# Two levels of Strassen for three quarters of the query projections, and values weighed by half blocks, in an attention kernel

## The chip, the core and the metric

The kernel runs on one core of a Trainium2 chip. The metric is device time in microseconds (us) of one launch. Engines: PE (TensorE matmul; PEld is its weight load, which overlaps it), DVE (VectorE), ACT (ScalarE), POOL (GpSimd), SP (SyncE, which here issues nearly all DMAs).

## What is computed

Eight batch entries of 256 tokens with 512 features, float32. After a layer norm, attention with 128 heads runs beside a gated FFN, and `x + s * g` is returned:

```python
c_q = x @ Wq_down                      # 512 -> 64
c_kv = x @ Wkv_down                    # 512 -> 64
q_c = (c_q @ Wq_up)                    # 128 heads of 4
q_r = (x @ Wq_rope)                    # 512 -> 128 heads of 64: the large projection
k_c, v_c = c_kv @ Wk_up, c_kv @ Wv_up  # 128 heads of 4 each
k_r = x @ Wk_rope                      # 64, shared by all heads
scores = (q_c . k_c + q_r . k_r) / scale
out = softmax(scores) @ v_c            # then out @ Wo
```

The rope queries `q_r` are a product of 2048 x 512 with 512 x 8192; it and the scores are most of the work.

## The kernel before

All instructions are recorded in the order in which the Python runs (a manual schedule), so each engine's queue has exactly that order; semaphores are put in wherever a tile is written or read by another engine. A first phase does layer norm, the low-rank projections and the FFN gate for all tokens, block of 512 by block of 512, and writes gates, sums and projections to DRAM. Then a loop runs over 64 blocks `n`. A block is one batch entry and one group of 16 heads (`sg`); batch entries go in pairs (four pairs of 16 blocks). Each block has two halves. The text calls half 0 even and half 1 odd, and counts halves h = 2n + half, from 0 to 127.

What one half does, in the order in which it is recorded:

- `score` twice (line 864): 4 PSUM banks each, 48 matmuls of 256 columns in row tiles of 32. With it all eight banks are given out; banks come round in turn, and a bank's next user waits for its last reader.
- `Prepare` in every second even half: the small query and key projections of the next blocks (lines 249 to 261).
- `maxima` (877, DVE, eight reductions), `exponentials` (883, ACT, 16 in a half).
- `Project`: one unit j of the rope queries. A unit is a 256 x 512 weight part times the pair's 512 tokens, by one level of Strassen: seven products of two 128-row chunks, each on four column tiles of 32 (`on_columns`, line 173), 56 matmuls of 256 columns, into four banks. `first` gives four products, ACT copies them out between the exponentials of the second part (line 211), POOL adds them (`join`, 216 to 218), `second` accumulates three more onto the emptied banks, and DVE adds the last (`end`, 228 and 229). Unit j = h + 4 is made in half h, four to six halves before the scores that use it.
- `transpose` (890, DVE, eight), into `rings`, four tiles with three parts of half a block each.
- DMAs for later units: `load_rope` (124, 512 KB), and `sum_w`. For the first pair, `sum_w` adds the weights' four Strassen sums on POOL (136 to 139) and stores them to DRAM (`sums_d`, 140); later pairs load them (142, 512 KB). The sums of x are in DRAM (`xs_d`), and `load_xs` brings seven of them when a pair begins (167).
- In even halves: `spread` (269, POOL, masks the small queries of the next block), `normalize` (953 to 955, DVE), `weigh` of the block before (915: 32 matmuls of 256 columns over the whole block), `gather` of its result by ACT (936) with two adds on POOL in blocks with odd `sg` (942), and `place_values` (310, POOL, four copies).

The few lines that set the order in the middle of a half:

```python
pj.first()
for r, i in enumerate((0, 2, 3, 1)):
    exponentials(n, two, r)
    pj.take(i)
if pre:
    pre.take()
pj.join()
pj.second()
```

Of the kernel before, what the change touches and what calls it, by code (L numbers as in the profile page):

```python
# [32 lines left out]
EPS = 1e-5  # L33
QSCALE = float((HD + R) ** -0.5)
# [3 lines left out]
def mla_ffn_gate_kernel(  # L38
# [26 lines left out]
    ident = const.tile([P, P], F32, name="ident")  # L65
    make_identity(nc, ident)
# [18 lines left out]
    sums_d = [dram.tile([P, 4, 2, P], F32, name=f"sums_d{n}") for n in range(32)]  # L85
    gates_d = [dram.tile([P, D], F32, name=f"gate_d{n}") for n in range(NT // P)]

    actp = pool("act", 4)
    wp = pool("wrope", 2)
# [3 lines left out]
    wsp = pool("wsum", 2)  # L93
    xsp = pool("xsum", 1)
    qtp = pool("qt", 1)
# [10 lines left out]
    units = 4 * len(blocks) // 2  # L106
    ropes, wsums, xsums = {}, {}, {}
# [10 lines left out]

    def load_rope(j):

        if j < units:
            t = wp.tile([P, KT, 4 * R], F32, tag="w", name=f"w_{j}")
            sg, u = j // 4 % 8, j % 4
            nc.sync.dma_start(out=t, in_=w_rope[sg, u // 2][:, :, ds(u % 2 * 4 * R, 4 * R)])
            ropes[j] = t

    def sum_w(j):  # L130

        if j < units:
            t = wsp.tile([P, 4, 2, P], F32, tag="ws", name=f"ws_{j}")
            if j < 32:
                q = lambda a, k: ropes[j][:, 2 * k : 2 * k + 2, a::2]
                nc.gpsimd.tensor_add(t[:, 0], q(1, 0), q(1, 1))
                nc.gpsimd.tensor_sub(t[:, 1], t[:, 0], q(0, 0))  # L137
                nc.gpsimd.tensor_sub(t[:, 2], q(0, 0), q(1, 0))
                nc.gpsimd.tensor_sub(t[:, 3], q(0, 1), t[:, 1])
                nc.sync.dma_start(out=sums_d[j], in_=t)  # L140
            else:
                nc.sync.dma_start(out=t, in_=sums_d[j % 32])
            wsums[j] = t

    def sum_x(p, xnT):


        q = lambda k, e: xnT[:, 2 * k : 2 * k + 2, ds(e * S, S)]
        for i, of in ((0, q(0, 0)), (1, q(1, 0)), (2, q(1, 1))):
            nc.sync.dma_start(out=xs_d[p][:, i], in_=of)  # L150
        t = {i: xsp.tile([P, 2, S], F32, tag=f"x{i}", name=f"xt{i}_{p}") for i in range(3, 7)}
        for i, one, two in (
            (3, q(0, 1), q(0, 0)),
            (4, q(1, 1), t[3]),
            (5, q(1, 1), q(0, 1)),
            (6, q(1, 0), t[4]),
        ):
            nc.gpsimd.tensor_sub(t[i], one, two)
            nc.sync.dma_start(out=xs_d[p][:, i], in_=t[i])

    def load_xs(p):

        if p < B // 2:
            xsums[p] = {}
            for i in (0, 4, 5, 3, 1, 6, 2):
                xsums[p][i] = xsp.tile([P, 2, S], F32, tag=f"x{i}", name=f"x{i}_{p}")
                nc.sync.dma_start(out=xsums[p][i], in_=xs_d[p][:, i])
# [12 lines left out]
    class Project:  # L180


        def __init__(self, j):
# [3 lines left out]
            self.a = lambda a, k: w[:, 2 * k : 2 * k + 2, a::2]  # L187
            self.x = xsums[j // 32]
# [4 lines left out]
            self.banks = []  # L193
            self.e = [qtp.tile([P, S], F32, tag=f"e{i}", name=f"e{i}_{j}") for i in range(4)]
# [7 lines left out]
        def first(self):  # L202

            for i, (w, x) in enumerate(
                ((self.a(0, 0), 0), (self.s[:, 1], 4), (self.s[:, 2], 5), (self.s[:, 0], 3))
            ):
                self.banks.append(bank(f"q{i}_{self.j}")[:, 0:S])
                product(self.banks[i], w, self.x[x], True)

        def take(self, i):  # L210
            nc.scalar.copy(self.e[i], self.banks[i])  # L211

        def join(self):

            m1, m6, m7, m5 = self.e
            nc.gpsimd.tensor_add(m6, m6, m1)  # L216
            nc.gpsimd.tensor_add(m7, m7, m6)  # L217
            nc.gpsimd.tensor_add(self.out(1, 1), self.split(m7), self.split(m5))  # L218

        def second(self):  # L220

            for i, w, x in ((0, self.a(0, 1), 1), (2, self.a(1, 1), 6), (3, self.s[:, 3], 2)):
                product(self.banks[i], w, self.x[x], False)
            nc.scalar.copy(self.out(0, 0), self.split(self.banks[0]))

        def end(self):

            nc.vector.tensor_add(self.out(1, 0), self.split(self.e[1]), self.split(self.banks[2]))  # L228
            nc.vector.tensor_add(self.out(0, 1), self.split(self.e[1]), self.split(self.banks[3]))

        def start(self):
            self.first()
            for i in (0, 2, 3, 1):
                self.take(i)
            self.join()
# [78 lines left out]
    def first_phase(between):  # L314
        st = ExitStack()
        fw = pool("fw", 1, st)
        wdn_sb = fw.tile([P, KT, P], F32, name="wdn_sb")
# [389 lines left out]
        for tb in range(NTB):  # L707
            more = tb + 1 < NTB
            for u in range(6):
# [9 lines left out]
                if pj:  # L719
                    pj.second()  # L720
                    pj.end()
# [20 lines left out]
            else:  # L742
                low_out(tb, 2)
                low_sum(tb)
            gate_out(tb)
# [48 lines left out]
    def between(step):  # L794
# [4 lines left out]
        elif step == 1:  # L799
            load_act(0)  # L800
            load_act(1)
            for b in range(2):
                load_cv(b, qtp.tile([P, S], F32, tag=f"e{b}", name=f"cv_{b}"))
            for j in range(2):
                load_rope(j)
        elif step == 2:
            load_xs(0)
# [8 lines left out]
        elif step < 8:  # L816
            load_rope(step - 2)
            if step < 6:
                sum_w(step - 2)
        else:  # L820
            sum_w(4)
            sum_w(5)
            load_act(2)
# [20 lines left out]
    rings = [tp.tile([P, 3, 8, 4, 32], F32, name=f"ring{r}") for r in range(4)]  # L844
# [43 lines left out]
    def transpose(n, f, r):  # L888

        nc.vector.transpose(  # L890
            rings[r][:, (2 * n + f // 2) % 3].rearrange("p k q i -> p q k i")[:, ds(2 * (f % 2), 2)],
# [4 lines left out]
    swapped = {}  # L896

    def weigh(n, halves=range(2)):
# [3 lines left out]
        if 0 in halves:  # L902
            avs[n] = bank(f"av_{n}")
        av = avs[n]
        slots = [(2 * n + half) % 3 for half in halves]
        if len(slots) == 2:
            one, two = sorted(slots)
            of, cols = slice(one, two + 1, two - one), ds(0, S)
            swapped[n] = one != slots[0]
        else:  # L910
            of, cols = slice(slots[0], slots[0] + 1), ds(halves[0] * P, P)
            swapped[n] = False
        for k in range(8):
            for r in range(4):
                nc.tensor.matmul(  # L915
                    av[32 * r : 32 * r + 32, cols],
                    vpad[:, k, r, :],
                    rings[r][:, of, k].rearrange("p h q i -> p h (q i)"),
# [5 lines left out]
    def gather(n, cols=ds(0, S)):  # L924


        b, sg = blocks[n]
        if n not in accs:
            accs[n] = [
                smp.tile([P, S], F32, tag=f"acc{what}{sg % 2}{b % 2}", name=f"acc{what}_{n}", bufs=1)  # L930
                for what in range(2)
            ]
        for what in (1, 0):
            side = (sg + what) % 2
            for to, of in ((early, late), (late, early)) if swapped[n] else ((cols, cols),):
                nc.scalar.activation(  # L936
                    accs[n][what][:, to], avs[n][:, of], AF.Copy, scale=sides_sb[:, side : side + 1]
                )
        if sg % 2:
# [64 lines left out]
    for n, (b, sg) in enumerate(blocks):  # L1004
        for half in range(2):
            one, two = 2 * half, 2 * half + 1
            j = 2 * n + half + 4
# [14 lines left out]
            if j < units:  # L1022
                pj = Project(j)
                pj.first()
                for r, i in enumerate((0, 2, 3, 1)):
# [142 lines left out]
```

## Time and profile before

| | |
|---|---|
| median of 3 runs | 1974.92 us (1974.73 to 1974.92) |
| profiled execution, span | 1971.5 us |
| PE busy | 1960.1 us (99%) |
| DVE busy | 1578.2 us (80%) |
| ACT busy | 1099.8 us (56%) |
| POOL busy | 758.5 us (38%) |
| DMA, mean over the span | 95 GB/s, 187 MB |
| PE busy by line: products (173, q) | 870.8 us |
| PE busy by line: scores (864) | 769.3 us |
| PE busy by line: weighing (915) | 233.4 us |

The profiler took one execution; its span runs from the first to the last instruction. "Busy" is time in which at least one instruction of the engine ran; register, semaphore and DMA-issuing instructions aren't counted. Matmuls are pipelined, so a mean duration (379 ns for a record of 256 columns) is longer than the distance from one start to the next. Each float32 matmul of the program stands in the trace as two records. In groups by shape, `128*32 128x256` is a weight tile of 128 rows and 32 columns and 256 columns that stream past it.

### The profile page before, as it was taken

The numbers are of one execution on the slowest core, as the hardware profiler recorded it, in microseconds if no ns is written. First come the engines' busy times: TensorE is split into PE (matmuls) and PEld (weight loads), VectorE is DVE, ScalarE is ACT, GpSimd is POOL, SyncE is SP. The second block draws the span as 40 slices with busy tenths as digits, with TensorE's granted clock in tenths as the row PEclk, the third lists the DMA queues.
The fourth block names the chain that finished last, engine by engine and source line by source line (L and its number), as shares of the span: only waits on it lengthen the run. The fifth ranks groups of instructions, "written<-read, shape, count | busy, mean of one in ns | idle before, by whom it ended". The sixth has DMA issues, their size and how long they took to land.

```text
span 1971.5 us, 78641 instructions
## 1 busy us (share of the span) xinstructions
PE 1960.1 (99%) x34007; PEld 1308.5 (66%) x34007; DVE 1578.2 (80%) x2662; ACT 1099.8 (56%) x3031; POOL 758.5 (38%) x1113
## 2 busy tenths in 40 slices
PE   9999999999999999999999999999999999999998
PEld 4335677677677666676777766776776767677675
DVE  7765678888887877888887877788787878888888
ACT  4433565655665644656655654556656555655664
POOL 6867445455443233233233223232233323233232
PEclk9999999999999999999999999999999999999999
DMA  6344322222242223222232223222232222122212
GB/s 196 114 135 168 118 88 72 83 88 77 77 135 90 77 101 113 75 88 88 67 125 87 81 88 122 80 88 78 76 123 72 98 88 88 67 88 88 83 39 87
DMA packets 120078, 187.02 MB, mean 95 GB/s; under 512 B 10778, under 2 KB 84906, under 8 KB 119734
## 3 DMA queue, kind: packets, MB, share of 16 engines
q1 hardware_dynamic: 119665, 181.97, 27.3%
q8 instruction: 270, 4.42, 0.9%
q14 instruction: 75, 0.61, 0.1%
q0 software_dynamic: 64, 0.01, 0.0%
q10 hardware_dynamic: 4, 0.01, 0.0%
HBM read 147.86 MB, written 34.10 MB: 92 GB/s over the span
## 4 chain that ended last, share of the span: by engine, by line
PE 93%; POOL 2%; DVE 2%; DMA 1%; issue 1%; SPq 1%; ACT 0%; POOLq 0%; ACTq 0%; DVEq 0%
PE q L173 39%; PE sc L864 34%; PE av L915 11%; PE po L173 2%; PE pf L173 1%; PE py L173 1%; PE px L173 1%; PE qq L249 1%; DVE ring L890 1%; PE pm L173 1%; PE pp L173 1%; DMA wo_sb<-in_w_o_dram 0%; PE first L656 0%; PE vps L294 0%; DVE nmx L877 0%
## 5 line engine op out<-in xcount | busy, mean ns | idle before, releaser
L883 ACT ACTIVATE pr<-sc,nmx 128x256 f32<-128x256 f32 x2048 | 816.5, 501 | 462.8 <-DVE nmx L877 458.6
L877 DVE TENSOR_REDUCE nmx<-sc 128x2 f32<-128x512 f32 x1024 | 635.8, 684 | 282.2 <-PE sc L864 257.6
L890 DVE STREAM_TRANSPOSE ring<-pr 128x512 f32<-128x512 f32 x1024 | 635.1, 679 | 0.0
L216 POOL TENSOR_TENSOR e<-e,e 128x256 f32<-128x256 f32 x128 | 93.7, 732 | 1043.1 <-ACT e L211 559.3
L173 PE MATMUL q<-x,ws 128*32 128x256 f32 x8192 | 489.1, 379 | 0.1
L864 PE MATMUL sc<-act,qr 32*128 32x256 f32 x8192 | 488.4, 374 | 0.0
L864 PEld LDWEIGHTS sc<-act,qr 32*128 32x128 f32 x8192 | 420.9, 185 | 21.8
L173 PEld LDWEIGHTS q<-x,ws 128*32 128x32 f32 x8192 | 267.5, 110 | 175.0 <-POOL ws L137 0.6
L173 PE MATMUL q<-x,w 128*32 128x256 f32 x6144 | 381.7, 381 | 1.1 <-DMA x<-xs_d 1.1
L173 PEld LDWEIGHTS q<-x,w 128*32 128x32 f32 x6144 | 188.3, 110 | 154.9 <-ACT pr L883 35.5
L864 PE MATMUL sc<-kc,qcm 32*128 32x256 f32 x4096 | 280.9, 387 | 0.0
L864 PEld LDWEIGHTS sc<-kc,qcm 32*128 32x128 f32 x4096 | 198.1, 184 | 65.0 <-issue 54.1
L915 PE MATMUL av<-ring,vpad 128*32 128x256 f32 (+1 forms) x4160 | 233.4, 376 | 0.1
L211 ACT COPY e<-q 128x256 f32<-128x256 f32 x512 | 204.0, 399 | 29.9 <-PE q L173 29.7
L936 ACT ACTIVATE acc<-av,sides_sb 128x128 f32<-128x128 f32 (+1 forms) x172 | 60.7, 421 | 243.9 <-PE av L915 243.9
L915 PEld LDWEIGHTS av<-ring,vpad 128*32 128x32 f32 x4160 | 134.3, 110 | 88.7 <-issue 1.6
L269 POOL TENSOR_TENSOR qcm<-qc,mask_sb 128x1024 f32<-128x1024 f32 x64 | 122.3, 1911 | 0.0
L218 POOL TENSOR_TENSOR qr<-e,e 128x256 f32<-128x256 f32 x128 | 93.6, 731 | 10.0
L217 POOL TENSOR_TENSOR e<-e,e 128x256 f32<-128x256 f32 x128 | 93.6, 731 | 10.0
L310 POOL COPY vpad<-vall 32x128 f32<-32x128 f32 x256 | 75.5, 295 | 10.2 <-PE av L915 2.2
L228 DVE TENSOR_TENSOR qr<-e,q 128x256 f32<-128x256 f32 x128 | 54.0, 422 | 24.3 <-POOL e L216 17.4
L568 DVE SCALAR_TENSOR_TENSOR gate<-low,bcol_sb,px 128x512 f32<-128x512 f32 x44 | 32.8, 746 | 44.6 <-PE px L173 21.5
(134 smaller groups left out, 1137.2 us busy)
## 6 DMA issues: line engine op xcount, KB each, us to landing
w<-in_w_rope_dram SPq DMA_DIRECT2D x128, 512.0 KB
ws<-sums_d SPq DMA_DIRECT2D x96, 512.0 KB
sums_d<-ws SPq DMA_DIRECT2D x32, 512.0 KB
x<-xs_d SPq DMA_DIRECT2D x28, 256.0 KB
xt<-in_x_dram SPq DMA_DIRECT2D x16, 256.0 KB
xs_d<-xt SPq DMA_DIRECT2D x16, 256.0 KB
gate_d<-gs SPq DMA_DIRECT2D x16, 256.0 KB
g<-gate_d SPq DMA_DIRECT2D x16, 256.0 KB
```

The source lines that it names most:

```text
L173: nc.tensor.matmul(to[tile_], w[:, tile_], x, start=start, stop=stop, skip_group_check=True)
L211: nc.scalar.copy(self.e[i], self.banks[i])
L216: nc.gpsimd.tensor_add(m6, m6, m1)
L217: nc.gpsimd.tensor_add(m7, m7, m6)
L218: nc.gpsimd.tensor_add(self.out(1, 1), self.split(m7), self.split(m5))
L269: nc.gpsimd.tensor_mul(qcm, qks[b, sg // 2][0].rearrange("p (q i) -> p q i", i=32).unsqueeze(2).to_broadcast([P, 8, 4, 32]), mask_sb[:, ds ...
L310: nc.gpsimd.tensor_copy(vpad[rows, :, :, 8 * t + 4 * (sg % 2) :][..., :4], valls[b][rows, :, sg])
L864: nc.tensor.matmul(sc[r][:, h, :], lhs.rearrange("p t i -> p (t i)"), rhs, start=(part == 0 and h == 0), stop=(part == 2), skip_group_chec ...
L877: nc.vector.tensor_reduce(nmx[:, r, :], scs[n, f][r], AX.X, ALU.max, negate=True)
L883: nc.scalar.activation(p[:, h, :], scs[n, f][r][:, h, :], AF.Exp, bias=nmxs[n, f][:, r, h : h + 1])
L890: nc.vector.transpose(rings[r][:, (2 * n + f // 2) % 3].rearrange("p k q i -> p q k i")[:, ds(2 * (f % 2), 2)], prs.pop((n, f, r)).rearran ...
L915: nc.tensor.matmul(av[32 * r : 32 * r + 32, cols], vpad[:, k, r, :], rings[r][:, of, k].rearrange("p h q i -> p h (q i)"), start=(k == 0), ...
```

## The change

Three things go together.

1. **Two levels of Strassen for pairs 1 to 3.** Two units make a pair of units `m`; its product is split by Strassen twice: seven outer times seven inner products, 49 of 128 rows, 128 columns, on four column tiles each. Class `Twice` does it in two halves: part 0 has three outer products (21 of the 49), part 1 has four (28). Each inner product i is one call of `product(i)`, three banks in all; ACT takes results out (`take`), POOL adds through one scratch tile (`add_tmp`), DVE adds the third product (`add_bank`), and at the end of the half POOL makes the outer sums (`outer`). The first pair stays with `Project`, whose seven products are put in the same order of banks, j = h + 5 now.
2. **The second level's sums are made on the way.** In halves 0 to 23 of the loop an `aside` runs at the end of a half: `early_sums` (the last four first-level sums), `inner_x` (sums of x for a pair) or `inner_w` (sums of weights for one m). Each loads into the tile `staged`, adds in place on POOL, and stores to `w2_d` or `x2_d`. From half 25 on `load_w2` brings 256 KB for each product, seven products ahead, and `load_x2` the x sums of a pair. Weights, x sums, scratch and results of both classes share the slots of one tile, `mix`.
3. **Values are weighed by half blocks.** `weigh(n, half)` does 32 matmuls of 128 columns in the half after, in two pieces between the products; the rings have two parts instead of three, and `gather` runs in each half.

The diff, cut to what the text speaks of:

```diff
+BANK = {1: 0, 5: 1, 2: 2, 6: 0, 3: 1, 7: 0, 4: 0}
...
+    def raw_sums(q, to):
+        nc.gpsimd.tensor_add(to[0], q(1, 0), q(1, 1))
+        nc.gpsimd.tensor_sub(to[1], q(0, 0), q(1, 0))
+        nc.gpsimd.tensor_sub(to[2], to[0], q(0, 0))
+        nc.gpsimd.tensor_sub(to[3], q(0, 1), to[2])
...
+    def load_w2(n):
+        m, part, k = 16 + n // 14, n // 7 % 2, n % 7
+        if m < 64:
...
+                nc.sync.dma_start(out=to, in_=w2_d[m % 16][:, W_SUM[i], of])
...
+    class Twice:
+        def __init__(self, m, part):
+            self.m, self.part = m, part
+            self.n, self.count = 2 * (m // 2), (3, 4)[part]
...
+            self.t = slots(7, 6).rearrange("p (o c s) -> p o c s", o=6, c=4)
+            self.mine = self.t[:, 0:3] if part == 0 else self.t[:, 2:6]
+            self.tmp = slots(13)[:, 0 : self.count * P].rearrange("p (o s) -> p o s", s=P)
...
+        def product(self, i):
...
+            for o in range(self.count):
+                of = (w[:, 0:256:2], w[:, 257::2], w[:, 256::2])[o] if self.part == 0 else w[:, ds(o * P, P)]
+                on_columns(to[:, o], of, x[:, o], first and o == 0, True)
+            load_w2(n + NRING)
...
+        def take(self, i):
+            to = {1: self.mine[:, :, 0], 6: self.mine[:, :, 1], 4: self.mine[:, :, 2], 5: self.mine[:, :, 3]}
+            nc.scalar.copy(to.get(i, self.tmp), self.bank(i))
+        def add_tmp(self, c):
+            nc.gpsimd.tensor_add(self.mine[:, :, c], self.mine[:, :, c], self.tmp)
+        def add_bank(self):
+            nc.vector.tensor_add(self.mine[:, :, 1], self.mine[:, :, 1], self.bank(3))
+        def outer(self):
+            flat = [self.t[:, o].rearrange("p c s -> p (c s)") for o in range(6)]
+            def give_q(a, e, one, two):
...
+                nc.gpsimd.tensor_add(to, v(one), v(two))
+            one, four, two, seven, six, three = 0, 1, 2, 3, 4, 5
+            five = two
+            add = lambda i, j: nc.gpsimd.tensor_add(flat[i], flat[i], flat[j])
+            if self.part == 0:
+                give_q(0, 0, flat[one], flat[two])
+            else:
+                add(six, one)
+                add(seven, six)
+                give_q(1, 1, flat[seven], flat[five])
+                give_q(1, 0, flat[seven], flat[four])
+                add(five, six)
+                give_q(0, 1, flat[five], flat[three])
...
-    rings = [tp.tile([P, 3, 8, 4, 32], F32, name=f"ring{r}") for r in range(4)]
+    rings = [tp.tile([P, 2, 8, 4, 32], F32, name=f"ring{r}") for r in range(4)]
+    more["x2"] = pool("x2", 1).tile([P, 4 * SLOT + 7 * 384], F32, name="x2")
+    staged = more["x2"][:, 0 : 32 * P].rearrange("p (c m) -> p c m", c=4)
...
+    def inner_w(m):
+        for u in range(2):
+            j = 2 * m + u
+            for k in range(2):
+                to = staged[:, 2 * u + k]
+                nc.sync.dma_start(
+                    out=to[:, 0:512].rearrange("p (k m) -> p k m", k=2), in_=rope(j)[:, k::2]
+                )
+                nc.sync.dma_start(
+                    out=to[:, 512:1024].rearrange("p (o m) -> p o m", o=4), in_=sums_d[j][:, :, k]
+                )
+        q = lambda u, k: staged[:, 2 * u + k]
+        raw_sums(q, [q(1, 1), q(1, 0), q(0, 0), q(0, 1)])
+        nc.sync.dma_start(out=w2_d[m], in_=staged)
...
+    asides = dict(enumerate([(early_sums, j) for j in range(28, 32)]))
+    asides[4] = inner_x, 1
+    for h, m in zip((5, 6, 7, 8, 9, 10, 11, 12, 13, 15, 16, 17, 19, 20, 21, 23), (0, 1, 2, 3, 14, 4, 15, 5, 6, 7, 8, 9, 10, 11, 12, 13)):
+        asides[h] = inner_w, m
+    asides[14], asides[18] = (inner_x, 2), (inner_x, 3)
...
-            if j < units:
-                pj = Project(j)
-                pj.first()
-                for r, i in enumerate((0, 2, 3, 1)):
-                    exponentials(n, two, r)
-                    pj.take(i)
+            if h < 123:
+                tw = Project(j) if j < 32 else Twice(16 + (h - 27) // 2, (h - 27) % 2)
+                for i in (1, 5, 2):
+                    tw.product(i)
+                exponentials(n, two, 0)
+                tw.take(1)
+                tw.product(6)
+                exponentials(n, two, 1)
+                tw.take(5)
+                tw.product(3)
+                exponentials(n, two, 2)
+                tw.take(6)
+                tw.take(2)
+                tw.add_tmp(0)
+                if h:
+                    weigh(*back, range(4))
+                tw.product(7)
+                if h:
+                    weigh(*back, range(4, 8))
+                exponentials(n, two, 3)
                 if pre:
                     pre.take()
-                pj.join()
-                pj.second()
+                tw.take(7)
+                tw.add_tmp(3)
+                tw.product(4)
...
+            if tw:
+                tw.take(4)
+            if h:
+                gather(*back, back[0] < last)
             if half == 0:
                 if n < last:
                     spread(n + 1)
+                if n >= 1:
+                    place_values(n)
+            if tw:
+                tw.outer()
...
+            if j < 32:
+                sum_w(j + 1)
+                load_rope(j + 2)
+            if h in asides:
+                what, of = asides[h]
+                what(of)
+            if h == 25:
+                for k in range(4):
+                    load_w2(k)
```

Smaller edits: `ident` moves from the lasting tiles to those of the first phase; unit 4 is made at the end of the first phase (`pj = Project(4)`, before `gate_out`); the `acc` tiles of odd `sg` are shared by both batch entries of a pair; for h = 0 to 21 `sum_w` still adds on POOL, afterwards it loads what `early_sums` made.

## The prediction

> **What bounds the kernel now.** I read the page's busy times and chain first, then the trace in order of time over two halves of the loop, then rows by shape.
>
> ```profile
> PE 1960.1 (99%) x34007; PEld 1308.5 (66%) x34007; DVE 1578.2 (80%) x2662; ACT 1099.8 (56%) x3031; POOL 758.5 (38%) x1113
> ...
> PE 93%; POOL 2%; DVE 2%; DMA 1%; issue 1%; SPq 1%; ACT 0%; POOLq 0%; ACTq 0%; DVEq 0%
> ```
>
> PE is never without work and is nearly all of the chain. So less PE work is time, but only while nobody makes PE wait; POOL, at 38%, decides nothing yet. Two halves in order of time (start, us, engine, line):
>
> ```profile
> 999.97 1.15 PE L864 MATMUL sc<-kc,qcm 32*128 32x256 f32 x16
> ...
> 1003.65 3.77 ACT L883 ACTIVATE pr<-sc,nmx 128x256 f32<-128x256 f32 x10 [4.25 <-DVE nmx L877]
> 1005.36 1.07 PE L173 MATMUL q<-x,w 128*32 128x256 f32 x16
> ...
> 1007.28 0.41 ACT L211 COPY e<-q 128x256 f32<-128x256 f32 x1
> ...
> 1008.28 0.41 ACT L211 COPY e<-q 128x256 f32<-128x256 f32 x1
> ...
> 1011.43 3.64 PE L915 MATMUL av<-ring,vpad 128*32 128x256 f32 x64
> ...
> 1015.00 1.15 PE L864 MATMUL sc<-kc,qcm 32*128 32x256 f32 x16
> ...
> 1026.57 1.15 PE L864 MATMUL sc<-kc,qcm 32*128 32x256 f32 x16
> ```
>
> An even half (999.97 to 1015.00) is 15.03 us: scores 5.39, seven products 6.07, weighing 3.57. An odd one is 11.57. Every second even half also prepares (1.09, the qq and qk rows), so four halves are 54.3, 27.15 for two. ACT's first product copy starts 7.3 us into the half and the next 1.0 later. The two records of each of four column tiles are a "group"; 56 records of products are 14 groups of 256 columns, and inside a stretch they start every 0.4315 us (1008.84 minus 1006.25, over 6).
>
> ```profile
> 1949.31 1.95 PE L915 MATMUL av<-ring,vpad 128*32 128x128 f32 x64
> 1951.08 5.33 PE L173 MATMUL po<-wo_sb,outT 128*32 128x512 f32 x48
> ```
>
> Here are 8 groups of 128 columns: 1.77 us, start to start, 0.221 each. The PE part of the change is priced by this.
>
> **PE's part.** Two units together took 28 groups of 256 (12.08 us) and will take 49 groups of 128 (49 x 0.219 in the steady part of those records = 10.7): 1.37 less, for 48 pairs of units 66 us. Weighing by halves takes 16 groups of 128 for 8 of 256: 3.50 for 3.45, 3 us in all. If PE stays the bound, the run loses 63 us.
>
> **POOL's part in the late halves (27 to 122).** The rows for POOL:
>
> ```profile
> L269 POOL TENSOR_TENSOR qcm<-qc,mask_sb 128x1024 f32<-128x1024 f32 x64 | 122.3, 1911 | 0.0
> ...
> L942 POOL TENSOR_TENSOR acc<-acc,acc 128x256 f32<-128x256 f32 x62 | 45.9, 761 | 19.9 <-ACT acc L936 19.9
> ...
> L989 POOL TENSOR_TENSOR g<-g,xr 128x512 f32<-128x512 f32 x15 | 19.0, 1272 | 54.3 <-DVE g L988 39.9 <-issue 14.4
> L158 POOL TENSOR_TENSOR xt<-act 128x512 f32<-128x512 f32 x8 | 12.6, 1569 | 0.0
> ```
>
> An add of 512 is 1.28 us (bounds 0.96, half the 1024 row, and 1.57), of 384 about 1.0, between the 512 row and 0.76. Before, a unit asked three adds of 256 of POOL. Now two units ask four add_tmp and seven outer adds, and six outer adds stand together at the end of an even half (part 1). POOL takes that half's queue in order: last add_tmp 1.28, in every second block the two adds of gather (1.4), spread 1.91, place_values 1.35 (four of 0.295 and gaps), then the outer six, 6 x 1.28 plus gaps = 8.1. The last of them reads t[2], and the first copy (take(1)) of the next odd half writes t[0:3]: ACT must wait, and behind it PE, whose fourth product (6) goes into the bank that this copy empties.
>
> The walk, even half from its start: take(1) at 7.3 as before; a copy of 512 costs 0.2 more than one of 256 (594 against 399 ns), so the copies come every 1.2; take(2) ends at 10.7, add_tmp(0) at 12.05, take(7) at 12.7, product 4 at 13.7. That is the half (PE alone needs 13.4). POOL: 12.75 + 1.28 + 1.91 + 1.4 + 8.1 = 25.5, and 27.75 with gather's adds, which wait for ACT's copies of av at 14.9. In the odd half's own time that is 11.85 or 14.1, where the copy was wanted at 7.3 and PE was ready at 7.4. From the copy on: product 6 at +0.55, take(5) done +1.6, product 3, half of weighing, product 7 done at +3.85, add_tmp(0) done +4.1, take(7) +4.65, product 4 done +5.45. The odd half is 17.3 or 19.5. With preparation in every fourth even half (+0.75), eight halves are 129.1 against 108.6: 5.1 us for each of the 48 pairs, **+246 us** (PE's 66 saved are inside this). With adds of 0.96: +139; with 1.57: +344. ACT's wait also delays the transposes of DVE, but they end 1 us before the half does. Loads hide: 1.8 MB a half, seven products ahead, against 1 MB in 4.5 us below.
>
> After such a wait PE may be slow. At the start of the run 512 columns took 1089 ns, later 592:
>
> ```profile
> L173 PE MATMUL px<-xs,w_sb 128*32 128x512 f32 x352 | 46.1, 593 | 0.2 <-DVE gate L568 0.2
> ...
> L656 PE MATMUL first<-rows,others 2*128 2x512 f32 x4 | 3.7, 1089 | 2.2 <-POOL others L376 2.2
> ```
>
> No wait of 4 us in mid-run stands in this trace, so from both sides: nothing, or all 4.4 us of PE's work in the odd half after the wait at half pace; along the walk, where ACT paces part of it, that is 2.3. I take 2.3 in two odd halves of three, as the start row is the only one of a PE coming from rest: **+72 us** (0 to 110).
> [...]
>
> **The asides (halves 4 to 23).** While the first pair still runs by single Strassen, each of 19 halves prepares the second level for 1/16 of the weights (or for one pair's x): eight loads, 2.1 MB, four adds of 1024 on POOL, one store of 2.1 MB, all through the one tile "staged", so the next loads wait for the store. What a megabyte costs (columns: window, its us, PE, PEld, DVE, ACT, POOL busy, clock, DMA share, GB/s):
>
> ```profile
> 1012.00:1013.00 1.00, 1.00 (x28) 0.58 (x20) 1.00 (x3) 0.00 (x0) 0.92 (x2) 1.00 0.72 198
> 1013.00:1014.00 1.00, 1.00 (x24) 0.59 (x20) 0.96 (x4) 0.00 (x0) 1.00 (x2) 1.00 1.05 356
> 1014.00:1015.00 1.00, 1.00 (x21) 0.40 (x13) 1.00 (x1) 0.00 (x0) 0.98 (x1) 1.00 1.06 429
> ```
>
> These two loads (1 MB) were issued at 1010.81: 1.2 us until data move, then up to 360 to 430 GB/s. So the 2.1 MB store takes 1.2 + 5.3 = 6.5 to 6.9, and the loads with the weights' own 0.5 MB beside them 1.2 + 7.0 = 8.2. Adds of 1024: 2.35 each on the line through the 256 and 512 rows (1.91 by L269), four with gaps 9.7. One turn: 9.7 + 6.8 + 8.2 = 24.7, some 27 in even halves, where POOL's spread, place_values and sum_w (3.05, lines 136 to 139) outlast the store; 25.5 on average. PE can't run ahead: sum_w for a half stands in POOL's queue behind the aside of two halves before, and PE's second product needs it. A half of PE would be 13.55. From 4 to 21 that is 18 x (25.5 - 13.55) = 215, less 15 for the lead: **+200 us**. Bounds: turns of 22 (adds of 1.91, 430 GB/s) +137; of 29 (280 GB/s) +263. Early_sums in halves 0 to 3 (0.5 MB each way, 3 us of POOL) fit in a half.
>
> **Small parts.** A unit moves from half 123 to the first phase (+6); half 123 then lasts as long as DVE's reductions and transposes, 10.8 as in the last four now: together +4. A copy (product 5 into bank 1) delays product 3 by 0.1 at most in the early halves. ident's move and the acc tiles add no instruction. The rings lose their third part; weighing a half ends in the next half, 9 us before the transposes that write there again.
>
> **Sum.** Span 1971.5 + 246 + 72 + 200 + 4 = 2493.5; the median lies 3.4 above the profiled span: 2497 us.
>
> **Rivals.**
> - *PE stays the bound* (7%): 1971.5 - 63 + 4 + 3.4 = 1916 us, faster. It needs the outer adds done by 7.3 us of the odd half, 4.5 earlier than the walk has them: six adds in 3.6 us, 0.6 each; and staging within 13.5. For it: POOL has 62% idle time. Against: every row of POOL, and the order of the queue.
> - *One of the two costs is absent* (19%): staging overlaps more than I see, 2497 - 200 = 2297; or the copy doesn't wait (short stalls of 0.5 to 1 us remain, as take(1) ends 0.45 after PE is ready), 1971.5 - 63 + 45 + 200 + 4 + 3.4 = 2161.
> - *Weight loads bind too* (8%): PEld is busy 1.68 of the 1.77 us of the 128-column stretch. The other one (1956.23 to 1958.48) ran at 0.281 a group, probably waiting for DVE. At that pace 49 groups are 13.8, 3 us more per pair, on the path in both halves: +144, 2641 us.
> - That the change doesn't do what it says is not seen: 49 groups and half weighings stand in the code.
>
> **Numbers.** The forecast, both waits present, has 66%: 2497 us. Bounds 137 to 263, 139 to 344 and 0 to 110 are not all at an end together: 2230 to 2660, which takes in the third rival and the upper half of the second. About 0.2% (4 us) can be told from no change; faster 7%, within 1%, slower 92%.
>
> **What would show it.** In the profile after: ACT's copy in odd halves idle on POOL for 4 to 7 us; PE's idle time before the products (on_columns) put to ACT (late) and POOL (early), PE's share near 77%; halves 5 to 21 of about 25 us with POOL waiting for DMA; late pairs of halves near 32. Wrong: odd halves under 14 us, POOL's adds of 512 under 0.8, or loads that start before the store has landed.

## The result and the profile after

The changed kernel takes 2592.8 us (median of 4 runs, 2590.2 to 2599.12) against 1974.91 before: 1.3136 times as long, 95% interval 1.3118 to 1.3155. The forecast was 2497 us, its range 2230 to 2660. The profiled execution of the changed kernel spans 2589.7 us; before it was 1971.5, so 618 us are to be explained.

Two parts of its page: busy times, then the chain that ended last, by engine.

```profile
PE 2081.8 (80%) x46103; PEld 1644.3 (63%) x46103; DVE 1568.1 (61%) x2566; ACT 1259.3 (49%) x3211; POOL 1317.9 (51%) x1365
...
PE 32%; POOL 25%; ACT 9%; DVE 3%; DMA 3%; issue 3%; SPq 2%; POOLq 0%; ACTq 0%; DVEq 0%
```

PE is busy for 80% of the span instead of 99%, and the chain has 32% on PE instead of 93%; POOL has a quarter, though it is busy for only half of the time. The chain's shares are of the span and add up to 77%: it could be followed back only to 593.6 us, into the asides, so it says little of the time before. An engine that is idle half the time sets the pace: it is late at certain places. The list of waits says which (who waits, for whom, us in total, times, longest):

```profile
PE r L201 <- ACT mix L361: 238.8, 52, 6.6
ACT mix L361 <- POOL qr L377: 225.2, 47, 6.2
...
PE q L201 <- POOL mix L160: 211.4, 21, 16.6
...
POOL x L160 <- DMA x<-sums_d: 197.4, 15, 14.4
```

The first two lines are one wait seen twice: in 47 late odd halves ACT's first copy (361) waits for POOL's last outer sum (377), and PE's fourth product waits for that copy. The last two are the early wait: PE's second product waits for `sum_w`, which stands in POOL's queue behind an aside (160 also does its adds), which waits for the aside's loads. 239 + 211 = 450 us of PE's idle time have these two names.

The table is a count from the traces, from the span's start and from each half's first score to the next half's, in us (halves 24 to 26 stand alone because the first weights of the new part are loaded there):

| | loop starts | 0 to 3 | 4 to 23 | 24 to 26 | 27 to 122 | rest |
|---|---|---|---|---|---|---|
| before | 208.1 | 50.1 | 269.3 | 41.6 | 1330.9 | 71.5 |
| changed | 231.5 | 60.1 | 531.4 | 52.3 | 1646.6 | 67.8 |
| difference | +23.4 | +10.0 | +262.1 | +10.7 | +315.7 | -3.7 |

A late odd half in order of time (start, us, engine, line, operation, in brackets the idle time before it and its releaser):

```profile
1493.14 2.17 PE L201 MATMUL r<-x,mix 128*32 128x128 f32 x72
1493.37 2.63 POOL L381 TENSOR_TENSOR mix<-mix 128x512 f32<-128x512 f32 x2
...
1496.09 2.50 POOL L377 TENSOR_TENSOR qr<-mix 128x512 f32<-128x512 f32 x2
1498.54 1.26 POOL L381 TENSOR_TENSOR mix<-mix 128x512 f32<-128x512 f32 x1
1499.88 1.26 POOL L377 TENSOR_TENSOR qr<-mix 128x512 f32<-128x512 f32 x1
1501.17 0.48 ACT L361 COPY mix<-r 128x384 f32<-128x384 f32 x1 [6.06 <-POOL qr L377]
...
1501.70 2.79 PE L201 MATMUL r<-x,mix 128*32 128x128 f32 x48 [6.39 <-ACT mix L361]
```

POOL works without a pause; it only began late. Six outer sums end at 1501.14, ACT copies, PE goes on 6.39 us after its third product. And it goes on slowly: 48 records take 2.79 us, where the 72 before the wait took 2.17. The granted clock of the same stretch (columns: window, its us, PE, PEld, DVE, ACT, POOL busy, clock, DMA share, GB/s):

```profile
1496.50:1497.50 1.00, 0.00 (x0) 0.00 (x0) 1.00 (x3) 0.00 (x0) 1.00 (x2) 1.00 0.82 288
1497.50:1498.50 1.00, 0.00 (x0) 0.00 (x0) 1.00 (x3) 0.00 (x0) 1.00 (x1) 0.77 0.55 164
1498.50:1501.70 3.20, 0.00 (x0) 0.00 (x0) 0.20 (x1) 0.53 (x2) 2.56 (x3) 0.50 0.12 37
1501.70:1504.40 2.70, 2.69 (x52) 2.46 (x56) 0.71 (x1) 2.70 (x8) 0.00 (x0) 0.50 0.02 3
...
1504.80:1505.20 0.40, 0.40 (x20) 0.40 (x16) 0.40 (x2) 0.20 (x1) 0.40 (x1) 0.92 0.86 302
```

Here the clock falls to one half some 2.7 us after the last product (1495.3) and is whole again 3.1 us after work came back. Over the late halves it fell in 45 of the 48 odd ones, 2.1 to 5.4 us after the last product, and came back 2.6 to 6.0 us after the next; PE worked 186 us at half clock.

An aside, from one turn's adds to the next (SPq is SP's queue of DMAs):

```profile
465.10 2.35 POOL L160 TENSOR_TENSOR x<-x 128x1024 f32<-128x1024 f32 x1 [13.46 <-DMA x<-sums_d]
...
474.74 0.33 SPq L1031 DMA_DIRECT2D w_d<-x  x1
...
479.43 6.03 PE L201 MATMUL q<-mix 128*32 128x256 f32 x64 [14.37 <-POOL mix L160]
...
482.46 0.80 SPq L1023 DMA_DIRECT2D x<-in_w_rope_dram  x1
...
493.62 2.38 POOL L160 TENSOR_TENSOR x<-x 128x1024 f32<-128x1024 f32 x1 [12.15 <-DMA x<-sums_d]
```

From adds to adds it is 28.5 us here: adds until the store is issued 9.6, the store until SP can issue the next loads 7.7, loads until the adds begin 11.2. All three go through the one tile `staged`, one after the other. In the turn shown SP's queue held the loads up: the store of `sum_w` ahead of them waited for POOL until 481.48. In about half of the turns it is the store's landing instead, 6 to 7 us after its issue.

### The profile page after: what moved, and what is told of

Read it like the earlier page. It is cut to its first block, busy times and chain, and to the rows that moved or that the text cites. A ratio compares the mean times of both kernels' runs of the same rounds, so it can differ in the third digit from the quotient of the medians.

```text
span 2589.7 us, 103880 instructions
## 1 busy us (share of the span) xinstructions
PE 2081.8 (80%) x46103; PEld 1644.3 (63%) x46103; DVE 1568.1 (61%) x2566; ACT 1259.3 (49%) x3211; POOL 1317.9 (51%) x1365
## 4 chain that ended last, share of the span: by engine, by line
PE 32%; POOL 25%; ACT 9%; DVE 3%; DMA 3%; issue 3%; SPq 2%; POOLq 0%; ACTq 0%; DVEq 0%
PE sc L1070 12%; PE r L201 11%; POOL qr L377 7%; POOL mix L381 7%; PE av L1112 5%; ACT mix L361 5%; ACT pr L1089 3%; POOL qcm L424 3%; DVE nmx L1083 3%; POOL mix L364 3%; PE po L201 2%; POOL vpad L465 2%; DMA x<-sums_d 1%; PE q L201 1%; POOL acc L1146 1%
## 5 line engine op out<-in xcount | busy, mean ns | idle before, releaser
L201 PE MATMUL r<-x,mix 128*32 128x128 f32 x14208 | 502.4, 300 | 238.8 <-ACT mix L361 238.8
L201 PEld LDWEIGHTS r<-x,mix 128*32 128x32 f32 x14208 | 425.6, 121 | 298.9 <-ACT mix L361 253.2
L364 POOL TENSOR_TENSOR mix<-mix 128x384 f32<-128x384 f32 x192 | 219.7, 1144 | 730.0 <-ACT mix L361 722.4
L361 ACT COPY mix<-r 128x512 f32<-128x512 f32 (+1 forms) x576 | 310.1, 569 | 459.3 <-POOL qr L377 225.2
L201 PE MATMUL q<-mix 128*32 128x256 f32 x3584 | 264.9, 446 | 247.3 <-POOL mix L160 211.4
L1112 PE MATMUL av<-ring,vpad 128*32 128x128 f32 x8192 | 298.1, 290 | 2.9 <-issue 1.8
L377 POOL TENSOR_TENSOR qr<-mix 128x512 f32<-128x512 f32 x192 | 242.0, 1272 | 33.2 <-POOL mix L364 25.7
L381 POOL TENSOR_TENSOR mix<-mix 128x512 f32<-128x512 f32 x144 | 183.2, 1272 | 7.7
L201 PE MATMUL r<-mix 128*32 128x128 f32 x4608 | 160.9, 275 | 8.1 <-issue 5.3
L201 PEld LDWEIGHTS r<-mix 128*32 128x32 f32 x4608 | 125.0, 110 | 31.9 <-ACT mix L361 21.9
L258 DVE TENSOR_TENSOR qr<-mix,q 128x256 f32<-128x256 f32 x32 | 13.2, 412 | 211.5 <-PE q L201 211.4
```

The costliest lines, as they stand in the source:

```text
L201: nc.tensor.matmul(to[tile_], w[:, tile_], x, start=start, stop=stop, skip_group_check=True)
L361: nc.scalar.copy(to.get(i, self.tmp), self.bank(i))
L364: nc.gpsimd.tensor_add(self.mine[:, :, c], self.mine[:, :, c], self.tmp)
L377: nc.gpsimd.tensor_add(to, v(one), v(two))
L381: add = lambda i, j: nc.gpsimd.tensor_add(flat[i], flat[i], flat[j])
L1112: nc.tensor.matmul(av[32 * r : 32 * r + 32, 0:P], vpad[:, k, r, :], rings[r][:, half, k].rearrange("p q i -> p (q i)"), start=(k == 0), st ...
```

## Experiments

A time here is that of one execution; the kernel before, run beside them, took 1973.6 to 1974.5 us. The differences are tens to hundreds of us, and each is read in its own stage. The stages of all runs, in us, where the changed kernel has 231.5, 531.4 and 1646.6 (the expectations count the loop's start from a point some 10.6 us before the span's: their 242 is 231.5 here, their 236 is 225.4):

| run | time | loop starts | 4 to 23 | 27 to 122 |
|---|---|---|---|---|
| outer sums first | 2407.62 | 231.7 | 532.6 | 1456.9 |
| asides in two pieces | 2533.71 | 229.3 | 486.5 | 1640.3 |
| PE kept at work | 2546.59 | 231.4 | 532.2 | 1598.6 |
| single Strassen throughout | 2029.31 | 231.3 | 271.9 | 1362.4 |
| aside's adds left out | 2420.53 | 229.5 | 375.3 | 1645.0 |
| joined | 2255.80 | 223.5 | 398.6 | 1459.2 |
| joined, aside's adds left out | 2216.01 | 223.8 | 359.8 | 1458.1 |
| joined, VectorE takes a share | 2347.46 | 223.4 | 445.7 | 1501.0 |
| joined, three outer sums left out | 2160.51 | 223.8 | 399.8 | 1365.1 |

### Outer sums first

```diff
             if tw:
                 tw.take(4)
+                tw.outer()
+            if half == 0 and n >= 1:
+                place_values(n)
             if h:
                 gather(*back, back[0] < last)
-            if half == 0:
-                if n < last:
-                    spread(n + 1)
-                if n >= 1:
-                    place_values(n)
-            if tw:
-                tw.outer()
+            if half == 0 and n < last:
+                spread(n + 1)
```

The same instructions, in another order on POOL.

> In even late halves POOL's queue now has the six outer adds first, then place_values, gather's adds and spread; no work is left out. If the late loss is the wait of the odd half's first copy for the last outer add in the order of POOL's queue: the adds end 3.3 us (4.7 with gather's adds) sooner, near 22.4 us after the even half's start, the copy starts at 8.7 us of the odd half instead of about 12 to 14, PE waits under 2 us and keeps full clock, odd late halves are 14 to 15 us instead of 20, and the run is about 2330 us. If instead the amount of POOL's work, or the wider copies of ACT, set the pace, nothing moves: the same instructions run, and the time stays near 2590.

Measured: 2407.62 us, 185 less; the late halves lost 190, the other stages stayed within 4. The copy of an odd half now:

```profile
1622.15 1.26 POOL L377 TENSOR_TENSOR qr<-mix 128x512 f32<-128x512 f32 x1
...
1623.45 0.48 ACT L361 COPY mix<-r 128x384 f32<-128x384 f32 x1 [1.36 <-POOL qr L377]
...
1623.98 0.86 PE L201 MATMUL r<-x,mix 128*32 128x128 f32 x24 [1.70 <-ACT mix L361]
```

The wait of 6.06 us became 1.36 and PE's 6.39 became 1.70. Odd halves went from 19.95 to 15.97 us on average; 13 of the 48 are near 14.2 (12.9 to 14.4), most of the others 15.5 to 15.9, and those with the output projection or the values' projections 16.6 to 19.2, which the expectation left out. The order alone, with not one instruction less, was worth 190 of the 316 us.

### Asides in two pieces

`inner_w` in two pieces of 512 columns, each with its four loads, its adds and its store.

```diff
+        for part in range(2):
+            cols = ds(512 * part, 512)
...
+            raw_sums(q, [q(1, 1), q(1, 0), q(0, 0), q(0, 1)])
+            nc.sync.dma_start(out=w2_d[m][:, :, cols], in_=staged[:, :, cols])
```

> inner_w loads, adds and stores the two 512-column halves of the staged tile one after the other, so that one half's adds run beside the other's store; bytes and elements are the same. If the early loss is the serial turn of load, four adds and store through one tile (27.8 us in the profile after), the turn falls to some 20 us and the run by about 135 us, to 2455. If the early loss is DMA bandwidth (5.2 MB a turn, 190 GB/s) or POOL's work, the turn stays at 27 and the run near 2590.

Measured: 2533.71 us; halves 4 to 23 lost 45 us, a third of what was expected. The turn, from one first store to the next, went from 28.2 to 25.1 us on average. The first store does start earlier, but the loads of the next turn are still recorded behind it in the next half, after the store of `sum_w` and `load_rope` in SP's queue, and POOL still waited some 9 us for them each turn.

### PE kept at work

Forty matmuls of 256 columns into the idle bank of the weighed values, in late odd halves, where PE waits for the copy; nothing reads them.

```diff
                 exponentials(n, two, 0)
                 tw.take(1)
+                if j >= 32 and half:
+                    avs[back] = bank(f"av_{back[0]}_{back[1]}")
+                    for k in range(10):
+                        on_columns(avs[back][:, 0:S], wo_sb[:, k % 4, 0:P], acts[b][:, 0, :], True, True)
                 tw.product(6)
```

> In odd late halves PE does 40 extra matmuls of 256 columns (10 groups, 4.3 us) into the idle av bank between products 2 and 6, where it waits; their result is overwritten. If the clock that falls to 0.50 in the wait costs time, the granted clock of late halves returns to 1.00, odd halves fall from 20.0 to about 18.4, and the run by some 70 us to 2520. If ACT's copies and POOL's adds pace the rest of the odd half, the clock rises but the time stays at 2590, or rises by up to 20 us where the wait is shorter than the extra work.

Measured: 2546.59 us; the late halves lost 48 us, 42 of them in the odd ones (0.9 each). The gain is net: 11 of the 48 odd halves became longer, by up to 3.3 us (in the first of them, where there was no wait to fill). PE has more to do and is done earlier. ACT's wait for POOL is as long as ever, what follows it is not:

```profile
1481.54 4.50 PE L201 MATMUL av<-act,wo_sb 128*32 128x256 f32 x80
...
1487.58 0.48 ACT L361 COPY mix<-r 128x384 f32<-128x384 f32 x1 [6.10 <-POOL qr L377]
...
1488.11 0.86 PE L201 MATMUL r<-x,mix 128*32 128x128 f32 x24 [2.07 <-ACT mix L361]
```

24 records take 0.86 us, where 48 took 2.79. The time at half clock in the late halves fell from 276 to 27 us (eight odd halves still have 3.4 us of it), and the granted clock of the whole run rose from 0.895 to 0.942. So the slow clock costs time of its own, 48 us net where the sum had 72. In the changed run the slow stretches of the late odd halves last 3.41 us (9 of them) or 6.83 (36), and fall and return come at different distances from the work, 2.1 to 5.4 and 2.6 to 6.0 us. PE was not always idle before a fall: in the 3.41 us ahead of it PE was busy for up to 38% of the time (last section).

### Single Strassen throughout

The changed program with `Project` for all pairs (7 products of 256 columns), no asides and no second level; banks' order, weighing by halves and the first phase as in the change.

```diff
-                tw = Project(j) if j < 32 else Twice(16 + (h - 27) // 2, (h - 27) % 2)
+                tw = Project(j)
...
-            if h in asides:
-                what, of = asides[h]
-                what(of)
```

> The kernel after, but every pair by single Strassen (Project) and without the asides: half-block weighing, the new order of products, the shared slots and unit 4 in the first phase remain. If the loss is all in the second level, this is within 30 us of the kernel before: 1971.5 plus 24 for the first phase as in the profile after, less 6 for the moved unit, plus 3 for weighing, about 1995. If half-block weighing or the new order costs by itself, it is well above, by some 0.5 us per half, 2050 or more.

Measured: 2029.31 us. So the second level with its preparation loses some 560 us, and the rest of the change some 56: 23 at the loop's start, 31 in the late halves, 5 in halves 0 to 23, less 4 in the rest. The 31 do not stand in every half: most blocks take 26.64 us for their two quiet halves, 26.60 before, so neither the weighing by halves nor the new order costs anything there. They stand in some 20 of the late blocks. PE's waits in the late halves add up to 20 us: 7.8 for the loads of the sums, 6.6 for ACT's exponentials, and 5.1 for ACT's first copy, as here, where three products instead of four stand ahead of the first bank that is used again:

```profile
604.98 3.66 PE L201 MATMUL q<-mix 128*32 128x256 f32 x64 [1.28 <-ACT mix L249]
```

### The aside's adds left out

The four adds of `inner_w` are gone (the second-level weight sums are raw quarters); loads and store stay.

```diff
-        raw_sums(q, [q(1, 1), q(1, 0), q(0, 0), q(0, 1)])
```

> The four additions of inner_w are left out; its loads and its store stay, so the second-level weight sums are the raw quarters and the output isn't the reference's. If the turn is the sum loads + adds + store through one tile, it falls by 9.7 us, from 27.8 to about 18 (loads 11.2 + store 6.9), and halves 4 to 23 (16 of 20 halves have this aside) go from 531 to about 376: about 2440 us. If the DMA's bandwidth is the bound, with POOL beside it, nothing changes: 2590 us. If POOL is the bound (adds plus its other work of each half), the half becomes as short as PE's 13.6: halves 4 to 23 near 290, 2350 us.

Measured: halves 4 to 23 take 375.3 us, 376 had been worked out from "loads plus store". The adds stood fully on the path: 156 us, 9.8 for each of 16 turns. Neither POOL's amount of work nor the bandwidth set the turn but their sequence. The run came out 20 us under the expected 2440: halves 24 to 26 also lost 10 and the loop began 2 earlier, which the expectation had not counted.

### Joined

The order of the first experiment, the pieces of the second, and two further moves: loads of the next aside go into SP's queue directly behind the store of this one, and unit 4 comes after the gate's matmuls.

```diff
             if h in asides:
                 what, of = asides[h]
                 what(of)
+            if h in (3, 21) or (h in asides and h + 1 in asides and h >= 3):
+                what, of = asides[23 if h == 21 else h + 1]
+                (inner_w_load if what is inner_w else inner_x_load)(of)
...
-                pj = Project(4)
-                pj.start()
-                pj.finish()
             gate_out(tb)
+            if not more:
+                pj = Project(4)
+                pj.start()
+                pj.finish()
```

> This kernel joins three edits that act in different stages, so each is read in its own stage. (a) Outer sums ahead of the values' placing, as in the first experiment: halves 27 to 122 should stay at that run's 1457 us if the stages don't touch each other. (b) The asides in two pieces of 512 columns, and the loads of the next aside issued directly behind the store of this one, half a loop body earlier. My theory of the early stage is a ring of one tile (loads 11.2, adds 9.7, store 6.9 us = 27.8): with pieces and earlier loads a turn should fall from 25 us to about 20, halves 4 to 23 from 486 (pieces alone) to about 410. Rival: DMA bandwidth is the bound; then the turn stays near 25 and halves 4 to 23 near 486. (c) Unit 4 made after the gate's matmuls instead of before them: they then cover the 6.3 us that its second product waited for POOL; the loop should start near 236 us instead of 242. If the cost of the first phase is only the unit's own work, it stays at 242. Together about 2325 us.

Measured: 2255.8 us, and each stage within 3 us of what was expected or better: late 1459.2 (1457), early 398.6 (410), the loop's start 8.0 us sooner (6). The effects add up, so the stages hardly feed one another. SP's queue over one turn shows the loads directly behind the stores:

```profile
450.05 5.83 SPq L1034 DMA_DIRECT2D w_d<-x  x2
455.94 3.45 SPq L1025 DMA_DIRECT2D x<-in_w_rope_dram  x4
460.65 2.55 SPq L1027 DMA_DIRECT2D x<-sums_d  x4
```

336 of the 618 us are won back without taking out one add. The remaining 282 us over the kernel before (2253.8 against 1971.5, span to span) are 15 at the start, 9 in halves 0 to 3, 129 in 4 to 23 and 128 in the late halves.

### What is left early, and what is left late

Two kernels on top of the joined one: one without the adds of `inner_w` (as above), one without the three in-place adds of `outer` (queries of pairs 1 to 3 are then incomplete sums).

```diff
-                add(six, one)
-                add(seven, six)
...
-                add(five, six)
```

> The joined kernel without the additions of inner_w (loads and stores stay, the weight sums are raw quarters). It tells what still holds halves 4 to 23 of the joined kernel at 398.6 us. If POOL (8 adds of 1.28 = 10.2 us a turn beside about 6 of its other work a half), they fall to what PE needs, 13.6 a half plus the four inner_x and sum halves: near 300, and the run to about 2155 us. If the transfers (4.2 MB a turn and the weights' 1 MB, about 13 us at 400 GB/s, with the loads still waiting for the stores), it falls by less than 40.

> The joined kernel without the three in-place additions of outer (add(six, one), add(seven, six), add(five, six)); the four that write the queries stay, so the queries of pairs 1 to 3 are incomplete sums. POOL has 3 x 1.28 = 3.85 us less between an even late half and the first copy of the odd one. In the joined kernel that copy still waits 1.26 us for POOL and add_tmp is late behind the values' copies and the mask. If POOL's work is what still holds the odd halves, they fall from 16.0 us by 2 to 3.85, halves 27 to 122 from 1459 to between 1275 and 1365: about 2145 us for the run. Rival: ACT's and VectorE's own chain of a half holds them; then only the 1.3 us of the wait go, 48 x 1.3 = 62, and the late halves stay near 1397.

Without the aside's adds halves 4 to 23 lose 39 us, 398.6 to 359.8: just under the 40 that the rival with the transfers allowed, far from the 100 that POOL's would have been. 90 of the joined kernel's 129 us remain without the adds. Loads and stores still follow one another through the one tile; in the changed run the loads that waited for a store's landing came 6 to 7 us after its issue. No run took the two apart. Without three outer adds the late halves lose 94 us, to 1365.1, the weakest value that the theory "POOL still holds them" allows. Even so, with part of the work missing, the late halves are no shorter than the 1330.9 before: a quiet odd half takes 12.8 us and a quiet even one 13.9, 26.7 together against 26.6 before. The 66 us that PE was to save were collected in no run.

### VectorE takes a share

The joined kernel, with VectorE making the second piece of each `inner_w` and two of the six outer sums.

```diff
-            raw_sums(q, [q(1, 1), q(1, 0), q(0, 0), q(0, 1)])
+            raw_sums(q, [q(1, 1), q(1, 0), q(0, 0), q(0, 1)], (nc.gpsimd, nc.vector)[part])
...
-                give_q(1, 1, flat[seven], flat[five])
-                give_q(1, 0, flat[seven], flat[four])
+                give_q(1, 1, flat[seven], flat[five], nc.vector)
+                give_q(1, 0, flat[seven], flat[four], nc.vector)
```

> As the joined kernel, and in addition VectorE makes the second piece of each weight aside and two of the six outer sums of the late even halves (512 columns each, some 1.0 to 1.6 us by the vector rows whose operands both lie in SBUF). If POOL's amount of work is what is left in both stages, halves 4 to 23 fall from about 410 to about 340 and halves 27 to 122 from 1457 to about 1400: some 2200 us. Rival: VectorE, 12 us busy of 14 in a late half, becomes the late bound, or the two engines slow each other in SBUF; then the late halves grow above 1457 while the early ones gain less than 40.

Measured: 2347.46 us, 92 slower than the joined kernel, and slower in both stages (445.7 and 1501.0): the theory was wrong, and the time went as the rival said. VectorE makes an outer sum in 688 ns against POOL's 1272, 1.85 times as fast. But its queue is in order, too:

```profile
1503.11 1.29 DVE L377 TENSOR_TENSOR qr<-mix 128x512 f32<-128x512 f32 x2 [4.04 <-POOL mix L381]
...
1503.88 1.65 POOL L381 TENSOR_TENSOR mix<-mix 128x512 f32<-128x512 f32 x1 [0.80 <-DVE qr L377]
...
1507.08 4.86 DVE L1087 TENSOR_REDUCE nmx<-sc 128x2 f32<-128x512 f32 x8
1507.79 3.75 ACT L1093 ACTIVATE pr<-sc,nmx 128x256 f32<-128x256 f32 x10 [6.93 <-DVE nmx L1087]
```

VectorE stands 4.04 us waiting for POOL; normalizing and the next half's maxima stand behind it, and ACT gets its first maximum 6.93 us after it was free, where that wait was 2.59 in the same half of the joined kernel. Over the late odd halves it is 5.5 us on average against 2.4. In the early halves VectorE waits for the loads in the same way (13 times, 120 us in all). The rival's other half is there too: the POOL sum beside VectorE's takes 1.65 us here instead of 1.27, and the 144 adds of line 381 take 1393 ns on average against 1285 in the joined kernel. How much of the loss each of the two makes was not separated. Here the faster engine made the kernel slower, because others depend on its queue.

No kernel tried comes near the 1974 us before.

## Why the prediction was right, and where its terms were not

**What bounds it (right).** Both waits that the prediction named are there, at its places: ACT's copy behind POOL's outer sums, 6.06 us in the half shown and 4.8 on average (4 to 7 were named), and POOL waiting for DMA in the asides. The outer sums take 1.27 us each, 1.28 was predicted. Order and pieces, changed separately, each took away their own stage's time.

**POOL's part and the slow clock (+246 and +72, measured +316 together).** The mechanism is right; that the sum fits to 2 us is luck. The clock's term took 2.3 us in two odd halves of three; keeping PE at work won 48 us net, 0.9 in each odd half. By an estimate, the 186 us that PE worked at half clock would cost 93 if PE alone set the pace; that ACT's copies pace part of that time is argued, not shown. The wait and the rest of the halves then make 268. Two things in the walk were wrong on the way. Its 27.15 us for a pair of halves before prepares in every second even half, but the trace has 16.1 us only in every fourth even half: eight halves are 107.5, not 108.6, and the term would have been 13 us larger. And it left out the output and the values' projections, which add 3.44 or 1.09 us to an odd half before, 41 us in all; in the changed kernel the 16 late odd halves with them average 22.0 us, the 32 without them 18.9, where the walk has 18.4. What is left over in the quiet halves, some 0.5 us each, the clock included, was not isolated. The granted clock shows the slow stretches in mid-run, 0.50 in the half above. Of the run's start, from whose rows the sum took its half pace, it shows nothing: the clock's record begins only 15.6 us after the span's start (13.2 in the changed run).

**The asides (+200, measured +262).** The mechanism was right: the turn is loads plus adds plus store, and without the adds the stage took 375.3 us where 376 follow from that. The mis-sized term is "the loads with the weights' own 0.5 MB beside them 1.2 + 7.0 = 8.2": they took 11.2 us. SP issues the eight loads one after the other over 5.7 us, about 0.6 to 0.9 each, so they do not all run from the beginning; and SP reached the first of them 7.7 us after the store was issued, behind the store of `sum_w` and `load_rope` (6.8 had been taken). The 15 us taken off for PE's lead don't show either: the eighteen halves 6 to 23 take 27.9 us on average. Adds (9.7, measured 9.6) were right. The upper bound of the turn, 29 us, held it.

**PE's part (-66).** The price of a group was right: 16 groups start every 0.220 us in each late even half, 0.219 was taken. But no run collected the gain: in the shortest late halves of the two-level kernels, those with three outer sums left out, PE still waits for ACT's copies in the odd halves (22 us in all); what makes up the rest was not isolated. In this step the prediction was right to put it inside the walk instead of adding it as a gain.

**Small parts (+4, measured about +40).** Three things were missed. Unit 4 in the first phase was priced at its own work (+6), but the loop starts 23.4 us later: its second product waited for POOL,

```profile
212.36 7.30 PE L201 MATMUL q<-mix 128*32 128x256 f32 x80 [6.29 <-POOL mix L160]
```

where `sum_w` stood behind the gated FFN's adds. After the gate's matmuls, as in the joined run, 8 us of it are gone; 15 remain. Halves 0 to 3 were said to have room for `early_sums` and lost 10. And in half 25 the sums' load stood in SP's queue behind the last aside's store:

```profile
853.64 4.96 PE L201 MATMUL q<-mix 128*32 128x256 f32 x64 [10.85 <-DMA mix<-sums_d]
```

With the asides shorter (joined), that half falls from 25.7 to 14.7 us. The first and the last are of one kind: an instruction priced by its duration, not by what stands ahead of it in its queue.

**The rivals.** PE as the bound: refuted, PE waits 450 us in the two places alone. One cost absent: refuted, both stages lost time. Weight loads as the bound: refuted, with no wait before them the 16 groups of a late even half start every 0.220 us, near the 0.219 of the sum and not 0.281.

## What to carry to other kernels

An engine that is busy half the time can set the pace. Read for each of its instructions who waits for it, and put what is waited for first: the same adds in another order gave back 190 us here, while the faster engine with its own queue gave back none. A preparation "on the side" through one tile costs the sum of its loads, work and store, and each DMA must be priced with the time until its queue reaches it (7.7 us in the turn shown); here the adds in it cost their full 9.8 us a turn. And this split, which saves columns on the bound engine, gives the others more small steps (copies, adds, DMAs): its gain of 66 us needs those steps to fit into halves of some 13 us, and they didn't.

## What the runs showed of the chip

- In the late halves of the changed run the granted clock changed 90 times, always whole multiples of 3.41 us apart. All 45 falls to 0.50 came after a stretch of this grid in which PE was busy for at most 38%; of 355 stretches at full clock without a fall behind them, two had PE busy for less than 45% (43 and 44%). Short waits did not keep the clock whole: with the outer sums first, where the weight loads of the late products waited for ACT's copies for 2.0 us at the longest, the granted clock of 1400 to 2200 us was 0.98 on average. (The ends of matmuls are modelled in the trace, so the shares are approximate.)
- Matmuls nobody reads cut the late halves' time at half clock from 276 to 27 us and made the run 46 us shorter, though PE had 3840 more records to do.
- In the run with VectorE's share, instructions of VectorE and POOL with two operands each in SBUF took longer beside one another, both or one of the two. The same add of 512 took VectorE 0.69 us alone and 2.27 beside POOL's mask, and POOL's mask 2.21 instead of 1.90; in the late half shown POOL's sum took 1.65 instead of 1.27, while VectorE's two took 1.29 together. Where VectorE's add took one operand from PSUM (line 367), POOL's add of 384 beside it (line 364) kept its time: in the changed run 1.01 us in 47 such cases and 1.00 in the 49 others. The slow pair and the add alone:

```profile
485.14 2.21 POOL L424 TENSOR_TENSOR qcm<-qc,mask_sb 128x1024 f32<-128x1024 f32 x1
485.63 2.27 DVE L161 TENSOR_TENSOR x<-x 128x512 f32<-128x512 f32 x1
...
514.12 0.69 DVE L161 TENSOR_TENSOR x<-x 128x512 f32<-128x512 f32 x1
```
